# Dequantized weights kept in DRAM as signed bytes, turned into 32-bit numbers on GpSimd

## The chip, the cores and the metric

The kernel runs on one core of a Trainium2 chip. The metric is the device time of one execution in microseconds (us); the profile's span is the time from the first to the last instruction of one profiled execution. A core has these engines, which work side by side, each through its own queue in order: TensorE (PE, the matmuls; its loads of weights are listed as PEld), VectorE (DVE), ScalarE (ACT), GpSimd (POOL), and SyncE (SP), which here issues nearly all DMAs. Matmuls write PSUM, which DVE and ACT read; the DMA engines move data between DRAM and the on-chip memory SBUF.

## The reference

The input is 2048 rows (tokens) of 1024 numbers. A feed-forward block of half weight, a state-space convolution and a second feed-forward block with the same weights follow one another, each behind a normalization and with its input added. The weights are 4-bit numbers, eight in a 32-bit word, with a zero point and a scale for every 128 rows:

```python
w = (qw[:, None, :] >> shifts[None, :, None] & MAXQ).reshape(-1, qweight.shape[1])
z = ((qz[:, :, None] >> shifts[None, None, :] & MAXQ) + 1).reshape(qzeros.shape[0], -1)
Wg, Wu, Wd = [(w - z[g_idx]) * s for each of gate, up, down]
...
x = x + 0.5 * (silu(ln(x) @ Wg) * (ln(x) @ Wu)) @ Wd
x = x + s4_convolution(ln(x))
x = x + 0.5 * (silu(ln(x) @ Wg) * (ln(x) @ Wu)) @ Wd
```

Gate and up are 1024 x 2752 each, down is 2752 x 1024, all in 32-bit floats.

## The kernel before

**Jobs.** The tokens are cut into four blocks of 512. Eight jobs (one block, first or second feed-forward each) run one after another, in the order of `JOBS`. A job has a gate/up stage (`gate_up`, 64 steps) and a down stage (`down`, 44 steps). The convolution of a block is hooked into the steps of the job after its first feed-forward.

**Gate/up.** The 2752 columns are cut into 21 pieces of 128 (the last of 64 columns), and these into eight waves: five of 3 pieces, three of 2. A wave has six accumulators in PSUM (four, or five at the end) and runs over the eight groups of 128 rows: one step is one wave and one group, with a weight tile of 128 x 768 (512 or 640). Each accumulator gets two matmuls a step, since the normalized input is kept as a high and a low part (`pieces`); the matmul of the low part takes the upper 16 bits of each 32-bit weight. After each group the accumulator is multiplied in place by the ratio of that group's scale to the next one's (`scaled`, L539 on ACT or L541 on DVE): this is called an eviction below. At the last group ACT applies silu, DVE multiplies by up (`hf`, a ring of two buffers, L600), and POOL splits the product into a high and a low part (`hh`, L602, and `hl`, L604).

**Down.** Two halves of 512 output columns, each over 22 pieces of rows, with four accumulators and two matmuls for each; evictions as above.

**Weights.** In the first job the packed words are fetched (`fetch`, `fetch_down`), split by DVE into two words of four 4-bit numbers in bytes each (`bytes_of`, L439 and L440), and DVE subtracts the zero points (a table of bf16 numbers, made by `zero_points`, spread to 128 rows by a DMA) from every fourth byte and writes 32-bit numbers `q` (`dequantize`, L454; `dequantize_down`, L486). SP writes `q` to DRAM (`w_q`, `wd_q`; L458, L488). The order of rows changes in this write: word row r holds the weights' rows 8r to 8r + 7. The first tile of all is also gathered directly from `q` by eight DMAs of POOL's queue (L457). `first_weights` hooks this into the steps: wave w is fetched three steps before step 8w - 12, split one step before it, and one eighth of it is dequantized in each step from there; the tiles of down follow from step 52 on into the down stage of job 0.

**Loads.** Every job reads all weight tiles from DRAM again (`load_w`, L523; `load_down`, L531), four steps ahead of use (`AHEAD`), into a ring of eight buffers `w` that is shared with `q`.

**Order.** The framework orders each engine's instructions by its own plan from the order of writing and the dependencies; `in_order_of_writing` forces the written order on named engines, as in `start` (the preparation ahead of the first matmul) and for the splits.

Of the kernel before, what the change touches and what calls it, by code (L numbers as in the profile page):

```python
# [9 lines left out]
F32 = mybir.dt.float32  # L10
BF16 = mybir.dt.bfloat16
F16 = mybir.dt.float16
I32 = mybir.dt.int32
U8 = mybir.dt.uint8
F32R = mybir.dt.float32r
AF = mybir.ActivationFunctionType
ALU = mybir.AluOpType
# [19 lines left out]
STEPS = [(w, g) for w in range(len(WAVES)) for g in range(GK)]  # L37
NH = HID // 512
LIFT = 2.0**20
NST = 64  # L40
# [12 lines left out]
def macaron_s4_kernel(  # L53
# [40 lines left out]
    hpool = ctx.enter_context(tc.tile_pool(name="h", bufs=2 * NF))  # L94
    wpool = ctx.enter_context(tc.tile_pool(name="w", bufs=8))
    gpool = ctx.enter_context(tc.tile_pool(name="g", bufs=3))
# [153 lines left out]
    s_dn = const.tile([P, NC, GD], F32, tag="s_dn", name="s_dn")  # L250
    z_dram = dpool.tile([2 * GK, INTER], BF16, tag="z", name="z_dram")
    zd_dram = dpool.tile([GD, HID], BF16, tag="zd", name="zd_dram")
    ok = const.tile([P, 8], F32, tag="ok", name="ok")
# [19 lines left out]
    def zero_points(which, z):  # L273

        p, n = z.shape
        zi = t2(f"zi_{which}").bitcast(I32)[:p, : 8 * n]
        for k in range(8):
            nc.vector.tensor_scalar(
                zi.rearrange("p (a k) -> p k a", k=8)[:, k, :],
                z,  # L280
                4 * k,
                15,
                ALU.logical_shift_right,
                ALU.bitwise_and,
            )
        tab = t2(f"ztab_{which}").bitcast(BF16)[:p, : 8 * n]
        nc.vector.tensor_scalar(tab, zi, 1.0, None, ALU.add)
        dst, seg, queue = (zd_dram, SEGD, nc.sync) if which else (z_dram, SEG, nc.scalar)
        queue.dma_start(dst.rearrange("g (s n) -> (g s) n", s=seg), tab)
# [15 lines left out]
    def scales(k0, k1, row):  # L305


        n = k1 - k0
        ps = bank(f"ps_s{k0}")
        u0, u1 = 2 * k0, 2 * k1  # L310
        for k in range(n):
            nc.tensor.transpose(
                ps[:, bass.ts(k, 2 * GK)], row[: 2 * GK, bass.ts(k, P)], ident[: 2 * GK, : 2 * GK]
            )
        if k1 == WIDE:
            row = t2("srow_half")
            for m, src in enumerate((gate_s, up_s)):
                nc.sync.dma_start(row[:GK, m * HALF : (m + 1) * HALF], src[:, WIDE * P :])
            nc.tensor.transpose(ps[:, bass.ts(2 * n, GK)], row[:GK, :P], ident[:GK, :GK])
            u1 = UNITS  # L320
        s = s_gu[:, u0:u1]
        flat = lambda a: a.rearrange("p u g -> p (u g)")
        nc.vector.tensor_copy(flat(s), ps[:, : (u1 - u0) * GK])
        inv = t2(f"inv_{k0}")[:, : (u1 - u0) * GK]
        inverse(inv, flat(s), k0)
        own = rat[:, u0:u1]
        inv = inv.rearrange("p (u g) -> p u g", g=GK)
        nc.vector.tensor_tensor(own[:, :, : GK - 1], s[:, :, : GK - 1], inv[:, :, 1:], ALU.mult)
        nc.vector.tensor_scalar(
            own[:, :, GK - 1 :], s[:, :, GK - 1 :], 1.0 / LIFT, None, ALU.mult  # L330
        )

    def scales_down():
# [16 lines left out]
        )  # L350
        nc.vector.tensor_scalar(ratd[:, :, GD - 1 :], s_dn[:, :, GD - 1 :], 0.5, None, ALU.mult)

# [43 lines left out]
    def units(w):  # L396
# [5 lines left out]
    w_q = [  # L402
        dpool.tile([HID, width_of(w)], F32, tag=f"wq{w}", name=f"wq{w}") for w in range(len(WAVES))
    ]
    wd_q = [dpool.tile([INTER, 512], F32, tag=f"wdq{a}", name=f"wdq{a}") for a in range(NH)]

# [11 lines left out]

    first_tile = wpool.tile([P, width_of(0)], F32R, tag="w", name="w_0_0")
    packed = {}  # L420
    NIBBLES = 0x0F0F0F0F

# [7 lines left out]
    def fetch_zeros(w):  # L430
        z = t2(f"z_{w}").bitcast(BF16)[:, : width_of(w)]
        for own, i, lo, hi in columns(w):
            src = z_dram[GK * i : GK * i + GK, lo:hi]
            nc.sync.dma_start(z[:, own], src.unsqueeze(1).to_broadcast([GK, 16, hi - lo]))
        packed[w][1] = z

    def bytes_of(raw, even):

        nc.vector.tensor_scalar(even, raw, NIBBLES, None, ALU.bitwise_and)  # L439
        nc.vector.tensor_scalar(raw, raw, 4, NIBBLES, ALU.logical_shift_right, ALU.bitwise_and)  # L440
        view = lambda a: a.bitcast(U8).rearrange("p (n k) -> p k n", k=4)
        return view(even), view(raw)

    def split(w):
        raw = packed[w][0]
        even = t4(f"even_{w}").bitcast(I32)[:, : width_of(w)]
        packed[w][0] = bytes_of(raw, even)

    def dequantize(w, j):

        parts, z = packed[w]
        q = wpool.tile([P, width_of(w)], F32R, tag="w", name=f"q_{w}_{j}")
        src = parts[j % 2][:, j // 2, :]
        nc.vector.tensor_tensor(q, src, z, ALU.subtract)  # L454
        dst = w_q[w].rearrange("(r j) n -> j r n", j=8)[j]
        if w == 0:
            nc.gpsimd.dma_start(first_tile[j:P:8].bitcast(F32), q[: P // 8].bitcast(F32))  # L457
        nc.sync.dma_start(dst, q.bitcast(F32))  # L458
        if j == 7:
            packed.pop(w)  # L460

    def fetch_down(a, rt):
# [4 lines left out]
        nc.sync.dma_start(both[:, 0], down_qw[rt * P : rt * P + n, cs])  # L467
        z = t4(f"zd_{a}_{rt}").bitcast(BF16)[:n, :512]
        g0 = 8 * rt
# [8 lines left out]
    def split_down(a, rt):  # L478
        both, z = packed[a, rt]
        packed[a, rt] = (bytes_of(both[:, 0], both[:, 1]), z)  # L480

    def dequantize_down(a, rt, j):
        parts, z = packed[a, rt]
        n = z.shape[0]
        q = wpool.tile([P, 512], F32R, tag="w", name=f"qd_{a}_{rt}_{j}")[:n]
        nc.vector.tensor_tensor(q, parts[j % 2][:, j // 2, :], z, ALU.subtract)  # L486
        rows = wd_q[a][8 * P * rt : 8 * P * rt + 8 * n]
        nc.sync.dma_start(rows.rearrange("(r j) n -> j r n", j=8)[j], q.bitcast(F32))  # L488
        if j == 7:
            packed.pop((a, rt))  # L490

    def first_weights(up, dn, at):


        for w in range(1, len(WAVES)):
            s0 = 8 * w - 12
            if w > 1:
                both = lambda w=w: (fetch(w), fetch_zeros(w))
                at(up, s0 - 3, lambda both=both: in_order_of_writing(both, ET.SP))
                at(up, s0 - 1, lambda w=w: in_order_of_writing(lambda: split(w), ET.DVE))  # L500
            else:
                at(up, 0, lambda: in_order_of_writing(lambda: split(1), *STARTING))
            for j in range(8):
                s = s0 + j if w > 1 else j // 2
                at(up, s, lambda w=w, j=j: dequantize(w, j))
# [9 lines left out]

    AHEAD = 4

    def load_w(j, s):
        if j == s == 0:
            return first_tile  # L520
        w, g = STEPS[s]
        t = wpool.tile([P, width_of(w)], F32R, tag="w", name=f"w_{j}_{s}")
        nc.sync.dma_start(t.bitcast(F32), w_q[w][bass.ts(g, P), :])  # L523
        return t

    def load_down(j, a, f):

        t = wpool.tile([P, 512], F32R, tag="w", name=f"wd_{j}_{a}_{f}")
        m = width(f)
        for o in range(0, P, m):  # L530
            nc.sync.dma_start(t[o : o + m].bitcast(F32), wd_q[a][f * P : f * P + m, :])  # L531
        return t

# [9 lines left out]
    def gate_up(j, b, hooks):  # L543
        hi, lo = pieces[b]
        ps = {}
        ready = {s: load_w(j, s) for s in range(AHEAD)}
        for s, (wi, g) in enumerate(STEPS):
            if s + AHEAD < len(STEPS):
                ready[s + AHEAD] = load_w(j, s + AHEAD)
            for hook in hooks.get(s, ()):  # L550
                hook()
            w = ready.pop(s)
            fs = WAVES[wi]
# [9 lines left out]
            for k, pos, done in turns:  # L563
# [18 lines left out]
                if g < GK - 1:  # L582
                    on_act = unit % 2 == 0 or (j == 0 and pos == 1)
                    if unit == 2 * WIDE:
# [37 lines left out]
    def down(j, b, hooks):  # L622

        steps = [(a, f) for a in range(NH) for f in range(NF)]
        ready = {d: load_down(j, *steps[d]) for d in range(AHEAD)}
        for d, (a, f) in enumerate(steps):
            if d + AHEAD < len(steps):
                ready[d + AHEAD] = load_down(j, *steps[d + AHEAD])
            for hook in hooks.get(d, ()):
                hook()  # L630
            w = ready.pop(d)
            if f == 0:
                ps = [acc(f"po_{j}_{a}_{c}") for c in range(4)]
            for c in range(4):
                for k, part in enumerate(reversed(h[f])):
# [7 lines left out]
                    )  # L643
                on_act = c % 2 == 0 or (j == 0 and c == 1 and f % 4 < 3)
                if f < GD - 1:
# [648 lines left out]
    def start():  # L1294
# [19 lines left out]
        moments(0, 1, then)  # L1314
        deviations(0, 1, -LIFT)
        for i in range(8):
            dequantize(0, i)
# [100 lines left out]
```

## Time and profile before

| what | us |
|---|---|
| median of three runs | 2207.82 (2206.94 to 2211.19) |
| the profiled execution's own time | 2209.4 |
| its span | 2207.6 |
| first matmul of job 0 | 29.3 |
| job 0, gate/up and down | 204.5 and 103.9 |
| job 1 to job 7 | 292.2, 277.2, 248.0, 248.0, 274.8, 274.7, 242.0 |

Jobs 1, 2, 5 and 6 hold the convolutions, job 1 also the making of its tables. Busy over the span: PE 2114.3 us (96%), PEld 1420.1, DVE 1702.9 (77%), ACT 1428.7 (65%), POOL 368.1 (17%). The core read 306.86 MB from DRAM and wrote 50.73 MB. In the profile's tables a row names the line, the engine, the operation and `out<-in`, then the count, the busy time and the mean duration. "w<-wq" is a load of a gate/up weight tile, "wd<-wdq" of a down tile, "pg" and "po" are the accumulators of the two stages. A busy PE need not be at its peak, since matmuls overlap; the pace of its steps tells more.

### The profile page before, as it was taken

The numbers are of one execution on the slowest core, as the hardware profiler recorded it, in microseconds if no ns is written. First come the engines' busy times: TensorE is split into PE (matmuls) and PEld (weight loads), VectorE is DVE, ScalarE is ACT, GpSimd is POOL, SyncE is SP. The second block draws the span as 40 slices with busy tenths as digits, with TensorE's granted clock in tenths as the row PEclk, the third lists the DMA queues.
The fourth block names the chain that finished last, engine by engine and source line by source line (L and its number), as shares of the span: only waits on it lengthen the run. The fifth ranks groups of instructions, "written<-read, shape, count | busy, mean of one in ns | idle before, by whom it ended". The sixth has DMA issues, their size and how long they took to land.

```text
span 2207.6 us, 28034 instructions
## 1 busy us (share of the span) xinstructions
PE 2114.3 (96%) x9524; PEld 1420.1 (64%) x9524; DVE 1702.9 (77%) x2803; ACT 1428.7 (65%) x2245; POOL 368.1 (17%) x389
## 2 busy tenths in 40 slices
PE   5888889999999999999999999999999999999998
PEld 3444565566877658755686558776587765865576
DVE  7777969777786877777877787867778677777776
ACT  5667777555764577666766667646676467766665
POOL 0223301222011230122102220112201122012310
PEclk9999999999999999999999999999999999999999
DMA  7768775434453545644655454534455354564443
GB/s 249 248 225 271 242 255 165 140 108 157 134 158 115 171 135 155 193 145 119 208 163 174 127 172 134 158 115 153 138 137 154 115 177 136 155 194 146 133 131 119
DMA packets 163669, 359.93 MB, mean 163 GB/s; under 512 B 22395, under 2 KB 27572, under 8 KB 163518
## 3 DMA queue, kind: packets, MB, share of 16 engines
q1 hardware_dynamic: 162670, 356.50, 52.1%
q8 instruction: 78, 1.28, 0.2%
q10 hardware_dynamic: 592, 1.16, 0.1%
q0 software_dynamic: 256, 0.39, 0.1%
q14 instruction: 73, 0.60, 0.1%
HBM read 306.86 MB, written 50.73 MB: 162 GB/s over the span
## 4 chain that ended last, share of the span: by engine, by line
PE 73%; issue 7%; DVE 5%; POOL 2%; ACT 1%; DVEq 0%; POOLq 0%; ACTq 0%
PE pg L572 42%; PE po L636 24%; PE pc L934 3%; PE pc L915 1%; POOL hl L604 1%; DVE pg L541 1%; PE pb L658 1%; PE pt L215 1%; DVE hf L600 1%; DVE po L541 1%; POOL hh L602 1%; PE st L215 1%; DVE qd L486 0%; PE s_k L854 0%; ACT g L597 0%
## 5 line engine op out<-in xcount | busy, mean ns | idle before, releaser
L539 ACT ACTIVATE pg<-pg,rat 128x512 f32<-128x512 f32 x1264 | 799.9, 661 | 489.3 <-PE pg L572 487.5
L541 DVE TENSOR_TENSOR pg<-pg,rat 128x512 f32<-128x512 f32 x1144 | 761.5, 694 | 180.9 <-PE pg L572 176.1
L572 PE MATMUL pg<-xTh,w 128*128 128x512 f32 x2752 | 874.2, 444 | 12.4 <-DVE pg L541 9.9
L572 PE MATMUL pg<-xTl,w 128*128 128x512 f16 x2752 | 737.8, 384 | 32.7 <-DVE pg L541 14.5
L572 PEld LDWEIGHTS pg<-xTh,w 128*128 128x128 f32 x2752 | 522.4, 190 | 192.6 <-DVE pg L541 24.3
L636 PE MATMUL po<-hl,wd 128*128 128x512 f32 x1344 | 540.5, 403 | 15.7 <-DMA wd<-wdq 7.5
L539 ACT ACTIVATE po<-po,ratd 128x512 f32<-128x512 f32 x670 | 438.1, 662 | 162.5 <-PE po L636 161.8
L636 PE MATMUL po<-hh,wd 128*128 128x512 f32 x1344 | 525.3, 392 | 0.0
L541 DVE TENSOR_TENSOR po<-po,ratd 128x512 f32<-128x512 f32 x610 | 420.9, 698 | 99.2 <-PE po L636 95.4
L572 PEld LDWEIGHTS <-w 128*128 128x128 bf16 x2752 | 227.8, 99 | 370.4 <-issue 186.1
L602 POOL CAST hh<-hf 128x512 fp32r<-128x512 f32 x168 | 109.4, 651 | 1530.7 <-DVE hf L600 976.1
L636 PEld LDWEIGHTS po<-hl,wd 128*128 128x128 f32 x1344 | 253.0, 188 | 92.1 <-DVE po L541 19.7
L636 PEld LDWEIGHTS po<-hh,wd 128*128 128x128 f32 x1344 | 253.6, 189 | 46.3
L604 POOL TENSOR_TENSOR hl<-hf,hh 128x512 fp32r<-128x512 f32 x168 | 222.9, 1327 | 13.4
L600 DVE SCALAR_TENSOR_TENSOR hf<-pg,rat,g 128x512 f32<-128x512 f32 x168 | 124.3, 749 | 90.6 <-ACT g L597 42.8
L597 ACT ACTIVATE g<-pg,rat 128x512 f32<-128x512 f32 x168 | 110.8, 687 | 48.7 <-PE pg L572 38.5
L178 DVE BATCH_NORM_STATS2 stats<-x 128x6 f32<-128x512 f32 x96 | 63.6, 677 | 1.1
L215 PE MATMUL pt<-ident,xn 128*128 128x128 f32 x256 | 42.6, 283 | 11.0 <-ACT xn L1286 11.0
L238 DVE TENSOR_TENSOR xTl<-pt,xTh 128x512 f16<-128x512 f32 x56 | 38.4, 690 | 14.2 <-ACT xTh L237 13.4
L660 DVE TENSOR_TENSOR x<-x,pb 128x512 f32<-128x512 f32 x64 | 43.2, 679 | 6.2 <-PE pb L658 6.0
L215 PEld LDWEIGHTS pt<-ident,xn 128*128 128x128 f32 x256 | 33.1, 145 | 21.8 <-ACT xn L1286 12.8
L237 ACT CAST xTh<-pt 128x512 fp32r<-128x512 f32 x56 | 33.0, 590 | 18.8 <-PE pt L215 18.6
(151 smaller groups left out, 816.9 us busy)
## 6 DMA issues: line engine op xcount, KB each, us to landing
w<-wq SPq DMA_DIRECT2D x319, 384.0 KB
wd<-wdq SPq DMA_DIRECT2D x336, 256.0 KB
w<-wq SPq DMA_DIRECT2D x128, 256.0 KB
w<-wq SPq DMA_DIRECT2D x64, 320.0 KB
x<-in_L_attn_u_dram SPq DMA_DIRECT2D x30, 512.0 KB
wq<-q SPq DMA_DIRECT2D x40, 384.0 KB
wdq<-qd SPq DMA_DIRECT2D x32, 256.0 KB
xs<-x SPq DMA_DIRECT2D x16, 512.0 KB
```

The costliest lines, as they stand in the source:

```text
L178: nc.vector.bn_stats(stats[:, t, i, :], x[b][t][:, bass.ts(i, 512)])
L215: nc.tensor.transpose(ps[:, bass.ts(k, P)], n[:, bass.ts(k, P)], ident)
L539: nc.scalar.activation(dst, src, AF.Copy, scale=sc)
L541: nc.vector.tensor_tensor(dst, src, sc.to_broadcast([P, TB]), ALU.mult)
L572: nc.tensor.matmul(p, weights, (lo, hi)[k][:, g, :], start=(g == 0 and not done), stop=(g == GK - 1 and done), skip_group_check=True,)
L597: nc.scalar.activation(g, pg, AF.Silu, scale=rat[:, 2 * f, GK - 1 :])
L600: nc.vector.scalar_tensor_tensor(hf, pu, last, g, ALU.mult, ALU.mult)
L602: nc.gpsimd.tensor_copy(hi, hf)
L604: nc.gpsimd.tensor_tensor(lo, hf, hi.bitcast(F32), ALU.subtract)
L636: nc.tensor.matmul(ps[c], w[:, bass.ts(c, P)], part, start=(f == 0 and k == 0), stop=(f == NF - 1), skip_group_check=True,)
L660: nc.vector.tensor_tensor(part, part, ps, ALU.add)
L934: nc.tensor.matmul(dst, lhsT, rhs, start=start, stop=stop, skip_group_check=True)
```

## The change

**Bytes.** `w_q` and `wd_q` hold signed bytes instead of 32-bit floats. A byte is eight times (weight minus zero point): -128 to 120. The factor 8 is taken out of the last group's scale (`EIGHT`).

**Zero points in packed form.** The table in DRAM holds 32-bit words whose four bytes each are 120 - 8 * z (z without the 1), so that bit patterns add without a carry. `bytes_of` leaves each 4-bit number in bits 3 to 6 of its byte. The new `signed` adds table and word as 16-bit numbers on DVE, and flips each byte's top bit with an exclusive-or; `take_zeros` and `split_down` call it for both halves of a tile. What is left for `dequantize` is to pick every fourth byte into a contiguous `q`: on POOL, and for six of the eight picks of wave 0 on DVE.

**Conversion.** A load now brings bytes (`load_bytes`, ring of six buffers `b`, four steps ahead, across stages and jobs), and `make_weights`, three steps ahead, turns them into 32-bit numbers (`w`, now a ring of five): on POOL, except the very first tile (DVE) and, in the gate/up stage of job 0, the groups 1, 2 and 5 (ACT).

**Evictions of job 0.** Those that had been given to ACT beyond the even ones are cut: of the unit at place 1 in gate/up only groups 0 and 4 stay on ACT, and in down none of unit 1.

```diff
-    wpool = ctx.enter_context(tc.tile_pool(name="w", bufs=8))
+    wpool = ctx.enter_context(tc.tile_pool(name="w", bufs=5))
+    bpool = ctx.enter_context(tc.tile_pool(name="bytes", bufs=6))
+    qpool = ctx.enter_context(tc.tile_pool(name="q", bufs=4))
...
-        tab = t2(f"ztab_{which}").bitcast(BF16)[:p, : 8 * n]
-        nc.vector.tensor_scalar(tab, zi, 1.0, None, ALU.add)
+        tab = t2(f"ztab_{which}").bitcast(I32)[:p, : 8 * n]
+        nc.vector.tensor_scalar(
+            tab.bitcast(U16).rearrange("p (n k) -> p n k", k=2),
+            zi.unsqueeze(2).to_broadcast([p, 8 * n, 2]),
+            -8.0 * 257,
+            120.0 * 257,
+            ALU.mult,
+            ALU.add,
+        )
...
-    first_tile = wpool.tile([P, width_of(0)], F32R, tag="w", name="w_0_0")
+    first_tile = bpool.tile([P, width_of(0)], I8, tag="b", name="b_0_0")
...
-    NIBBLES = 0x0F0F0F0F
+    NIBBLES = 0x78787878
...
-        z = t2(f"z_{w}").bitcast(BF16)[:, : width_of(w)]
+        z = t4(f"z_{w}").bitcast(I32)[:, : width_of(w)]
...
-        nc.vector.tensor_scalar(even, raw, NIBBLES, None, ALU.bitwise_and)
-        nc.vector.tensor_scalar(raw, raw, 4, NIBBLES, ALU.logical_shift_right, ALU.bitwise_and)
-        view = lambda a: a.bitcast(U8).rearrange("p (n k) -> p k n", k=4)
-        return view(even), view(raw)
+        nc.vector.tensor_scalar(even, raw, 3, NIBBLES, ALU.logical_shift_left, ALU.bitwise_and)
+        nc.vector.tensor_scalar(raw, raw, 1, NIBBLES, ALU.logical_shift_right, ALU.bitwise_and)
+        return even, raw
+
+    def signed(part, z):
+        both = part.bitcast(U16)
+        nc.vector.tensor_tensor(both, both, z.bitcast(U16), ALU.add)
+        nc.vector.tensor_scalar(both, both, 0x8080, None, ALU.bitwise_xor)
+        return part.bitcast(I8).rearrange("p (n k) -> p k n", k=4)
...
-        q = wpool.tile([P, width_of(w)], F32R, tag="w", name=f"q_{w}_{j}")
-        src = parts[j % 2][:, j // 2, :]
-        nc.vector.tensor_tensor(q, src, z, ALU.subtract)
+        q = qpool.tile([P, width_of(w)], I8, tag="q", name=f"q_{w}_{j}")
+        engine = nc.vector if w == 0 and j % 3 < 2 else nc.gpsimd
+        engine.tensor_copy(q, packed[w][j % 2][:, j // 2, :])
...
-        q = wpool.tile([P, 512], F32R, tag="w", name=f"qd_{a}_{rt}_{j}")[:n]
-        nc.vector.tensor_tensor(q, parts[j % 2][:, j // 2, :], z, ALU.subtract)
+        q = qpool.tile([P, 512], I8, tag="q", name=f"qd_{a}_{rt}_{j}")[:n]
+        nc.gpsimd.tensor_copy(q, src)
...
+    LOAD, MAKE = 4, 3
...
+    def make_weights(i):
+        j, stage, s = queue[i]
+        b = loaded.pop(i)
+        made[i] = t = wpool.tile(list(b.shape), F32R, tag="w", name=f"w_{stage}_{j}_{s}")
+        if i == 0:
+            nc.vector.tensor_copy(t, b)
+        elif j == 0 and stage == "up" and s % GK in (1, 2, 5):
+            nc.scalar.copy(t, b)
+        else:
+            nc.gpsimd.tensor_copy(t, b)
...
+    def next_weights():
+        i = at_use[0]
+        at_use[0] += 1
+        for k in range(LOAD) if i == 0 else ():
+            load_bytes(k)
+        for k in range(MAKE) if i == 0 else ():
+            make_weights(k)
+        if i + LOAD < len(queue):
+            load_bytes(i + LOAD)
+        if i + MAKE < len(queue):
+            make_weights(i + MAKE)
+        return made.pop(i)
...
-                    on_act = unit % 2 == 0 or (j == 0 and pos == 1)
+                    on_act = unit % 2 == 0 or (j == 0 and pos == 1 and g % 4 == 0)
...
-                on_act = c % 2 == 0 or (j == 0 and c == 1 and f % 4 < 3)
+                on_act = c % 2 == 0
...
         deviations(0, 1, -LIFT)
+        take_zeros(0)
         for i in range(8):
             dequantize(0, i)
```

## The prediction

> **What bounds the kernel now.** I read the strips of the page first, then the busy times by stage, then who TensorE (PE) waited for, then the costs of single instructions.
>
> ```profile
> PEclk9999999999999999999999999999999999999999
> DMA  7768775434453545644655454534455354564443
> ```
>
> DMA is at 6 to 8 tenths in the first six of 40 slices (55 us each) and at 3 to 6 afterwards: the first job, which also makes the weights, is another regime. So I cut the span at the jobs, whose bounds I found by counting matmuls in the timeline.
>
> ```profile
> core 0: us, PE busy (x) PEld busy (x) DVE busy (x) ACT busy (x) POOL busy (x), PEclk, DMA share, GB/s
> 0.00:29.30 29.30, 5.33 (x24) 3.86 (x25) 22.27 (x65) 12.41 (x19) 4.78 (x15) 0.92 0.70 231
> 29.30:233.80 204.50, 177.44 (x727) 98.00 (x728) 154.99 (x230) 143.95 (x236) 46.68 (x40) 0.95 0.75 253
> 233.80:337.70 103.90, 93.24 (x393) 68.42 (x393) 81.92 (x143) 74.35 (x122) 22.59 (x19) 0.97 0.75 241
> ...
> 907.10:1155.00 247.90, 244.29 (x1097) 162.25 (x1096) 192.54 (x304) 169.24 (x266) 39.33 (x42) 1.00 0.53 164
> ```
>
> Rows: preparation, gate and up of job 0, down of job 0, and the whole of job 3 with the same matmuls. Job 0 takes 308.4 us, job 3 247.9 us, of which PE is busy 244.3: later jobs are at PE's own pace (2.70 us for a step of 12 matmuls, 1.81 for one of 8). What can be won lies almost all in job 0: its first stage 204.5 against 162.6 in job 3 (some 3 us of the difference are job 0's own transposes), its second 103.9 against 85.6, so about 39 + 18 = 57 us. The waits of PE in job 0 (29.2 to 337.7), and after it:
>
> ```profile
> PE pg L572 <- DMA w<-wq: 13.9, 11, 3.8
> PE pg L572 <- DVE pg L541: 9.9, 7, 4.0
> PE po L636 <- DMA wd<-wdq: 7.5, 3, 5.0
> PE po L636 <- DVE po L541: 3.3, 7, 1.3
> PE pg L572 <- DMA w<-q: 2.7, 1, 2.7
> ```
> ```profile
> PE pg L572 <- DVE pg L541: 14.5, 25, 2.1
> ```
>
> Total us, times, longest. In job 0 the weights' DMAs hold PE for 13.9 + 7.5 = 21.4 us, VectorE (DVE) for 13.2; in the other seven jobs no DMA holds PE. The clock lost 0.05 x 204.5 + 0.03 x 103.9 = 13.3 us more: after the stop that ends at 134.4 us (3.5 us) the next twelve matmuls take 5.2 us in place of 2.7.
>
> **What one instruction costs.**
>
> ```profile
> L454 DVE TENSOR_TENSOR q<-even,z x32: 676/948/2021, 16.6 to 202.5; 128x768 fp32r<-128x768 uint8 x20, 128x512 fp32r<-128x512 uint8 x8, 128x640 fp32r<-128x640 uint8 x4
> L439 DVE TENSOR_SCALAR rawd<-rawd x6: 413/422/1503, 189.3 to 280.4; 128x512 int32<-128x512 int32 x4, 88x512 int32<-88x512 int32 x2
> L602 POOL CAST hh<-hf x168: 603/612/1346, 58.0 to 2115.2; 128x512 fp32r<-128x512 f32 x168
> L604 POOL TENSOR_TENSOR hl<-hf,hh x168: 1263/1280/2305, 58.7 to 2115.9; 128x512 fp32r<-128x512 f32 x168
> L730 DVE TENSOR_TENSOR s_cos<-s_dr 128x1024 f32<-128x1024 f32 x1 | 1.2, 1219 | 0.0
> ```
>
> ns min/median/max (the last row: busy us, mean ns).
>
> **1. Bytes in DRAM.** A gate/up tile falls from 384 to 96 KB, a down tile from 256 to 64, written once and read eight times. In job 0 every step reads and writes one, so most of the 253 GB/s goes. The 21.4 us of DMA waits go, and I credit about 60% of the lost clock to them (21.4 of some 35 us of waits): -8. In jobs 1 to 7 the gain is nothing: no DMA wait is there. Price: -29.4.
>
> **2. Conversion to 32 bits, added, mostly on GpSimd (POOL).** No row converts bytes. Nearest is the one-input cast: 0.612 us for 512 columns. From L604 (1.28 for 512) and L927 (1.00 for 384 columns, two inputs) an instruction has a fixed part near 0.18 us, so a cast runs at 0.84 ns a column: 0.83 us for 768. The other end is the two-input slope, 2.15 ns a column: 1.83 us.[...] A wave of eight steps in job 0 has 5 conversions and 8 byte picks on POOL and three pairs of casts at 1.89: by the row 13 x 0.83 + 5.7 = 16.5 us of PE's 21.6[...]. I take the row: one input, one output. In later jobs 8 x 0.83 + 5.7 = 12.3 of 21.6.
>
> Latency: in job 3 the last hl of a wave ends 8.46 us after the wave's last step begins; the conversion queued behind it is needed 11.3 us after, 9.3 where the next wave has 4 units. With 0.6 to 0.9 us it is in time. POOL's casts stand in the same queue: a conversion in front of hh and hl delays hl, and the two hf buffers pass that to DVE:
>
> ```profile
> DVE hf L600 <- POOL hl L604: 33.9, 29, 1.4
> ```
>
> That wait exists already. I take +1 us for all later jobs; the upper end is one conversion per wave on this path (second rival). A late conversion stops PE; a conversion on ScalarE (ACT; g = 1, 2, 5 of job 0, about 0.9 us) that waits for its bytes stops the evictions queued behind it. SP's order lends cover: loads are bound only by six byte buffers, each free once converted, except in job 0, where the load stands behind writes that wait for POOL's picks.
>
> **3. DVE in job 0.** Leaves: 56 + 48 subtractions, 56.2 + 38.1 = 94.3 us in the groups of that stretch. Comes: per half of each packed tile an add and an exclusive-or on 16-bit words, twice the columns. The row [...](L730: 1.22 for 1024) makes the add of 1536 words 1.75 us[...]; no row here shows 16-bit words, so both ends stay: over 7 waves and 6 down tiles 32 us[...] or 57 us. I take 32[...]. Evictions moved from ACT to DVE: 5 of 7 in each of 8 waves = 40, and 34 in down, 74 x 0.694 = 51. Contention: L439 goes from 422 to 1503 and L454 from 948 to 2021 where POOL works[...]. With POOL busy some 195 of 283 us (69 now, about 127 of new work at 0.84 ns a column and 0.18 us each), 80 such instructions wait about 0.25 us each (half a cast, two times in three): +20. Sum: -94 + 32 + 51 + 20 = +9. DVE was busy 237 of 308 us and would be 246 of about 283: it becomes the limit of job 0, and its 13.2 us of waits stay. I add +3 for the tighter fit.
>
> ACT loses 74 x 0.663 = 49 us and gains 22 to 24 conversions of 0.7 to 0.9: no limit.
>
> **4. Start.** The first matmul waits on this chain:
>
> ```profile
> 16.62 0.96 DVE L454 TENSOR_TENSOR q<-even,z 128x768 fp32r<-128x768 uint8 x1
> ...
> 29.29 1.44 PE L572 MATMUL pg<-xTl,w 128*128 128x512 f16 x3 [2.69 <-DMA w<-q]
> ```
>
> The zero table gets 688 outputs[...], +0.5; its 32-bit broadcast doubles those bytes, hidden behind bn_stats on DVE; add and or for two halves +2.9 to +5.4; eight subtractions of 0.87 become six copies of 0.55 to 0.95 on DVE, -3.7 to -1.3, two go to POOL, whose eight DMA issues (0.5 each) queue behind them; converting the first tile +0.5 to +0.95. Ends +0.2 and +5.6; I take +2.5.
>
> **Sum.** -29.4 + 1 + 3 + 2.5 = -22.9 on a span of 2207.6, whose run took 2209.4; the median is 2207.8, so the span stands for it: 2185, rounded to 2184.
>
> **Rivals.** *Job 0 reaches PE's pace*: conversions hide, DVE's words are cheap[...]: -57 + 2.5 gives 2153. For it: ACT has room, POOL is at 70%. Against: DVE at 246 of 253 us would need no gap. *POOL decides* (slower): at 1.22 us per 768 columns 13 conversions and picks plus casts fill 21.6 us. At 1.83, job 0 grows by 5 x 7.9 + 2 x 5.9 + 6 in its first stage and about 36 in down over a 253 us floor: 346, +38; later jobs lose about 2 us each at wave ends: 2260. The same end comes if conversions stand before hh and hl: 0.6 us in 56 waves = 34 us, which with the gain gives 2218. *DVE takes it all*: the 16-bit words run at the slow end (+25): 271 us of work in job 0 at 87% is 311: 2213. *Nothing moves*: the waits change from DMA to DVE at equal length: about 2207.
>
> **Chances.** Likeliest (2165 to 2200) 0.50; PE's pace 0.20; DVE takes it all 0.08; nothing moves 0.08; POOL decides 0.14. Range 2150 to 2232 leaves the far POOL case and a little below. About 4.4 us (0.2%) can be told from no change: faster 0.74, same 0.07, slower 0.19, a few of the "nothing" cases falling on either side.
>
> **What would show it.** Right: no PE wait on weight DMAs in job 0; DMA strip at 2 to 4; the conversion of 768 columns near 0.83 us; job 3 still near 248. Wrong: PE waiting for POOL's w after a wave's end, hf waiting longer for hl, the 16-bit add above 1.2 us, or first matmul after 35 us.

## The result, and the profile after

The changed kernel took 2196.07 us (median of four runs, 2195.57 to 2197.09), the kernel before 2208.9 (2206.94 to 2211.19): a ratio of 0.9939, 95% interval 0.9927 to 0.9952. The span of the profiled execution went from 2207.6 to 2193.7 us. About half of the forecast gain came. The repeated executions of one kernel differ in the clock granted to PE (a mean of 0.987 to 0.994 over the span in 23 executions of the kernel before, with times of 2204.3 to 2215.5 us), so a stage taken from one profile can hold a little more or less of lowered clock than another. The DMA strip of the page (PEclk is 9 in every slice, as before), and the stages, cut at the matmuls as before (preparation, gate/up of job 0, down of job 0, job 1, job 3):

```profile
DMA  4433321112111211211321121112111121121111
```
```profile
core 0: us, PE busy (x) PEld busy (x) DVE busy (x) ACT busy (x) POOL busy (x), PEclk, DMA share, GB/s
0.00:28.80 28.80, 4.65 (x19) 3.39 (x19) 19.90 (x54) 11.21 (x17) 7.16 (x17) 1.00 0.51 171
28.80:204.90 176.10, 170.55 (x732) 95.45 (x732) 149.72 (x255) 137.27 (x221) 127.48 (x161) 0.99 0.39 115
204.90:313.00 108.10, 97.06 (x395) 69.62 (x394) 91.94 (x176) 59.58 (x93) 63.97 (x89) 0.95 0.28 87
313.00:612.70 299.70, 291.64 (x1318) 196.59 (x1317) 240.56 (x409) 174.31 (x272) 121.41 (x158) 0.98 0.16 49
892.80:1140.10 247.30, 244.71 (x1097) 162.23 (x1096) 193.58 (x304) 169.35 (x266) 114.28 (x151) 1.00 0.20 61
```

Gate/up of job 0 fell from 204.5 to 176.1 us and its clock rose from 0.95 to 0.99. Down of job 0 *rose* from 103.9 to 108.1, although its DMA share fell from 0.75 to 0.28. Over the whole span, from the exact ends of the stages:

| part | change, us |
|---|---|
| before the first matmul | -0.5 |
| gate/up of job 0 | -28.4 |
| down of job 0 | +4.2 |
| gate/up of job 1, of job 2 | +7.0, +2.4 |
| down of jobs 1 to 7 (0.45 to 0.6 each) | +3.8 |
| gate/up of the other later jobs | -2.3 |
| after the last matmul | -0.2 |

The first two give 28.9 us, the rest takes back 15.0. The longest waits of PE in job 0 (total us, times, longest), then, from the groups by shape (busy us, mean ns), POOL's conversion and the 16-bit add in gate/up:

```profile
PE pg L628 <- DVE w_up L572: 6.6, 1, 6.6
PE pg L628 <- DVE pg L600: 3.3, 9, 0.6
PE pt L219 <- DVE xn L212: 2.7, 1, 2.7
PE po L689 <- DVE po L600: 2.7, 6, 1.1
PE po L689 <- ACT po L598: 2.1, 6, 0.6
PE po L689 <- DVE s_vc L758: 1.9, 1, 1.9
PE pg L628 <- POOL w_up L576: 1.5, 2, 0.8
PE po L689 <- POOL w_down L576: 1.4, 1, 1.4
```
```profile
L576 POOL CAST w_up<-b 128x768 fp32r<-128x768 int8 x304 | 255.7, 841 | 438.3 <-PE pg L628 337.5 <-issue 47.3 <-PE po L689 32.3
...
L461 DVE TENSOR_TENSOR even<-even,z 128x1536 uint16<-128x1536 uint16 x5 | 4.8, 952 | 0.8 <-DMA z<-z_dram 0.8
```

No weight DMA holds PE any more (6.6 is the start's own chain). In down, however, other stops have taken the place of the DMA's: `xn` (the normalized input of the next block, which PE transposes), evictions of DVE and of ACT, `s_vc` (one of the convolution's tables) and a conversion, 10.8 us in sum, where the weights' DMAs and the evictions had made 11.7 before. PE's busy time there grew from 93.2 to 97.1 us, at a clock of 0.95 in place of 0.97. Why down did not become shorter is the question for the experiments.

### The profile page after: what moved, and what is told of

It is laid out like the page before. It is cut to its first block, busy times and chain, and to the rows that moved or that the text cites. A ratio compares the mean times of both kernels' runs of the same rounds, so it can differ in the third digit from the quotient of the medians.

```text
span 2193.7 us, 29717 instructions
## 1 busy us (share of the span) xinstructions
PE 2119.6 (97%) x9524; PEld 1421.1 (65%) x9524; DVE 1720.4 (78%) x2826; ACT 1404.9 (64%) x2197; POOL 1015.0 (46%) x1334
## 3 DMA queue, kind: packets, MB, share of 16 engines
q8 instruction: 77, 1.26, 0.2%
## 4 chain that ended last, share of the span: by engine, by line
PE 84%; DVE 7%; POOL 4%; issue 2%; DMA 1%; SPq 1%; ACT 0%; POOLq 0%; DVEq 0%; ACTq 0%
PE pg L628 50%; PE po L689 26%; PE pc L987 3%; DVE pg L600 2%; PE pc L968 1%; PE pb L711 1%; POOL hl L660 1%; PE pt L219 1%; DVE po L600 1%; DVE hf L656 1%; POOL w_up L576 1%; PE st L219 1%; POOL w_down L576 1%; POOL hh L658 1%; DVE rawd L461 0%
## 5 line engine op out<-in xcount | busy, mean ns | idle before, releaser
L600 DVE TENSOR_TENSOR pg<-pg,rat 128x512 f32<-128x512 f32 x1184 | 788.0, 694 | 167.5 <-PE pg L628 163.2
L628 PE MATMUL pg<-xTh,w_up 128*128 128x512 f32 x2752 | 878.5, 444 | 11.9 <-DVE pg L600 9.4
L628 PE MATMUL pg<-xTl,w_up 128*128 128x512 f16 x2752 | 731.1, 384 | 14.7 <-DVE w_up L572 6.6
L576 POOL CAST w_up<-b 128x768 fp32r<-128x768 int8 (+2 forms) x487 | 376.0, 774 | 614.0 <-PE pg L628 470.6
L628 PEld LDWEIGHTS pg<-xTh,w_up 128*128 128x128 f32 x2752 | 519.7, 190 | 203.0 <-DVE pg L600 41.7
L689 PE MATMUL po<-hl,w_down 128*128 128x512 f32 x1344 | 540.6, 405 | 15.4 <-DVE po L600 9.7
L689 PE MATMUL po<-hh,w_down 128*128 128x512 f32 x1344 | 523.6, 393 | 0.0
L600 DVE TENSOR_TENSOR po<-po,ratd 128x512 f32<-128x512 f32 x640 | 441.6, 698 | 93.6 <-PE po L689 89.1
L628 PEld LDWEIGHTS <-w_up 128*128 128x128 bf16 x2752 | 228.3, 99 | 344.1 <-issue 165.2
L576 POOL CAST w_down<-bd 128x512 fp32r<-128x512 int8 x352 | 220.6, 628 | 422.3 <-PE po L689 366.2
L689 PEld LDWEIGHTS po<-hl,w_down 128*128 128x128 f32 x1344 | 252.9, 189 | 94.1 <-DVE po L600 23.9
L689 PEld LDWEIGHTS po<-hh,w_down 128*128 128x128 f32 x1344 | 254.0, 189 | 46.0
L660 POOL TENSOR_TENSOR hl<-hf,hh 128x512 fp32r<-128x512 f32 x168 | 218.0, 1297 | 7.9
```

The source lines that it names most:

```text
L576: nc.gpsimd.tensor_copy(t, b)
L600: nc.vector.tensor_tensor(dst, src, sc.to_broadcast([P, TB]), ALU.mult)
L628: nc.tensor.matmul(p, weights, (lo, hi)[k][:, g, :], start=(g == 0 and not done), stop=(g == GK - 1 and done), skip_group_check=True,)
L660: nc.gpsimd.tensor_tensor(lo, hf, hi.bitcast(F32), ALU.subtract)
L689: nc.tensor.matmul(ps[c], w[:, bass.ts(c, P)], part, start=(f == 0 and k == 0), stop=(f == NF - 1), skip_group_check=True,)
```

## The experiments

Each kernel is the changed one with the edit shown. Ratios are against the kernel before, on the same chip. One caution holds for all: the framework plans the order of instructions anew for each variant, and stages that an edit does not touch move with it. From here on a stage or job is counted to the end of its last matmul, which makes down of job 0 108.2 us and job 1 299.9 in the changed kernel. Where no edit touched it and `hf` had two buffers, down of job 0 took 106.7 to 108.6 us in three kernels, but job 1 296.0 to 301.7 in five. (The run with the traffic, left out of this band, adds copies in job 0 alone and still had 307.6 in job 1.) A stage is read against these bands. As to whole times, the intervals of the first two runs and of the run on the tables' order overlap the changed kernel's 0.9927 to 0.9952; those of the two runs that take work off POOL in down do not.

### Is it the evictions moved to DVE?

```diff
-                on_act = c % 2 == 0
+                on_act = c % 2 == 0 or (j == 0 and c == 1 and f % 4 < 3)
```

> Only the evictions of job 0's down stage go back to ScalarE as before the change (34 of them). Theory (VectorE is the bound of that stage, since the change gave it these evictions[...]): down of job 0 falls from 108.1 us to about 100, the span by about 8 us to 2186. Rival (that stage waits for GpSimd's queue, picks and conversions being late): it stays within 2 us of 108.

2190.1 us, ratio 0.9905 (0.9875 to 0.9935); down of job 0 106.3 us. That is 2 us less, at the edge of the band, not the 8 that the theory of overfull evictions wants, and within the rival's 2 us. The test is not clean, though: the new plan also put more of job 1's table instructions into DVE's queue in this stage (15.8 us in place of 7.3), and PE's waits there for DVE's evictions rose from 2.7 to 11.0 us. So the theory is not supported, and not refuted either.

### Are job 1's conversions on POOL what makes it longer?

```diff
-        elif j == 0 and stage == "up" and s % GK in (1, 2, 5):
+        elif (j == 0 and stage == "up" and s % GK in (1, 2, 5)) or (
+            j == 1 and stage == "up" and s < 44
+        ):
             nc.scalar.copy(t, b)
```

> Conversions of job 1's gate/up steps 0 to 43 (while the convolution's tables are made on VectorE) go to ScalarE in place of GpSimd. Theory[...]: job 1 falls by about 6 us from 299.7, its small VectorE operations e, r and s_work fall back from 16.6 us in sum to about 10, and the GpSimd hl operations go back to 1.28 us. Rival (job 1 lost its 7 us because the tables' instructions are planned in another order): no change beyond 2 us.

2191.64 us, ratio 0.9917 (0.9887 to 0.9947); job 1 297.8, 2 us less. Inconclusive: inside the band. The theory's own signs hardly came either: in job 1 the small instructions on `e`, `r` (128x4) and `s_work` (128x8) fell from 16.4 to 14.7 us, not to 10 (11.0 before the change), those on `r` stayed at 3.8, and the slowest `hl` still took 2.33 us. The same edit was tried again on another base below.

### Is the packed form needed?

```diff
-EIGHT = 8.0
+EIGHT = 1.0
...
-        packed[w] = [signed(part, z) for part in parts]
+        pass
...
-        engine = nc.vector if w == 0 and j % 3 < 2 else nc.gpsimd
-        engine.tensor_copy(q, packed[w][j % 2][:, j // 2, :])
+        nc.vector.tensor_tensor(q, parts[j % 2][:, j // 2, :], z, ALU.subtract)
```

Bytes and conversions stay; DVE subtracts a bf16 table from each eighth, as before the change.

> Bytes in DRAM and conversion as in the changed kernel, but the zero points are subtracted by VectorE byte by byte as before (112 instructions with 0.95 or 0.68 us), in place of the packed add and exclusive-or (52 instructions in the steps of job 0, 49 us) and GpSimd's picks. Theory (VectorE bounds job 0): 40 us more on VectorE, job 0 grows from 284 us to 305 to 325. Rival (job 0 is bound by GpSimd's queue or by DMA): job 0 stays at 280 to 290, or falls since GpSimd has 70 us less.

2212.57 us, ratio 1.0013 (1.0005 to 1.0021); job 0 190.1 + 115.0 us. The stretch of job 0:

```profile
26.60:331.80 305.20, 272.52 (x1125) 156.78 (x1125) 273.25 (x463) 196.69 (x315) 128.21 (x145) 0.98 0.31 92
```

DVE is busy for 273 of 305 us, against 241.7 of 284.3 in the changed kernel. So bytes without the packed form gain nothing with these evictions: the packed form is worth 0.0074 of the time, some 16 us.

### Does the traffic matter?

```diff
+    def extra(i):
+        n = 576 if queue[i][1] == "up" else 384
+        for k in range(2):
+            r = ((2 * i + k) % 16) * P
+            nc.sync.dma_start(extra_dram[k, i, :, :n], u[r : r + P, :n])
...
+        if queue[i][0] == 0:
+            extra(i)
```

Two unused copies from DRAM to DRAM per step of job 0, about the bytes that the change had saved.

> The changed kernel with two copies inside DRAM added to each step of job 0 (295 KB each in gate/up, 197 KB in down), which brings the DMA engines' bytes back to those of before; nobody waits for them. Theory (the weights' traffic was what held TensorE): TensorE waits for loads again and job 0 grows by 15 to 30 us from 284. Rival (the gain came from the other division of work between the engines): under 5 us.

2265.91 us, ratio 1.0245 (1.0212 to 1.0277). The two stages of job 0, then PE's waits there:

```profile
34.50:247.60 213.10, 176.00 (x731) 97.92 (x731) 149.95 (x252) 139.62 (x222) 119.56 (x150) 0.95 0.81 246
247.60:374.90 127.30, 100.03 (x392) 74.35 (x392) 90.51 (x146) 58.89 (x91) 65.62 (x97) 0.89 0.70 201
```
```profile
PE po L698 <- POOL w_down L576: 28.8, 15, 7.5
PE pg L637 <- POOL w_up L576: 19.9, 7, 5.8
```

The DMA share is back near 0.75 (0.81 and 0.70), the clock back at 0.95 and below, and job 0 is 56 us longer. Sign right, size missed: 15 to 30 had been expected. Each such copy reads and writes DRAM and stands in SP's queue ahead of a byte load, so it is more than a restoration. The reading to keep: a late DMA is now booked under POOL, whose conversions in turn waited 32.6 + 23.5 us for their bytes in this job; the name of the releaser changes, the cause does not.

### Is it POOL beside DVE in down?

POOL has two kinds of new or old work in down of job 0: the conversions, and the turn of the next block (`xTh`, `xTl`, L238 and L239), which the kernel gave to POOL in job 0 already before. One run takes each away.

```diff
-        elif j == 0 and stage == "up" and s % GK in (1, 2, 5):
+        elif j == 0 and (stage == "down" or s % GK in (1, 2, 5)):
             nc.scalar.copy(t, b)
```

> The 44 conversions of job 0's down stage go from GpSimd to ScalarE (busy 60 of 108 us there, then about 87). Theory (VectorE's packed add and exclusive-or of the down tiles, means 1.09 and 0.83 us against minima of 0.68 and 0.41, wait for GpSimd[...], and the evictions behind them hold TensorE): their means fall below 0.9 and 0.65, and down of job 0 falls from 108 to about 101. Rival (only the lump of these instructions ahead of the evictions counts, whatever GpSimd does): means and stage stay within 2 us.

2189.92 us, ratio 0.9902 (0.9885 to 0.9918); down of job 0 100.8, as the theory wants. Its signs came only by half: the exclusive-or's mean fell from 829 to 660 ns, but the add's rose from 1090 to 1168.

```diff
-                pool = j == 0
+                pool = False
```

> In the down stage of job 0 the transposed input's two parts are made by ScalarE and VectorE as in the other jobs (8 more VectorE instructions of 0.69 us) in place of GpSimd's cast and two-input subtraction (17.6 us). Theory[...]: the means of the packed add and exclusive-or of down fall by 0.1 us or more each, and the stage stays within 3 us of 108 since VectorE gets 5.5 us more and 3 to 5 us of waits less. Rival (no conflict): means unchanged, the stage 4 to 6 us longer.

2188.22 us, ratio 0.9897 (0.988 to 0.9913); down of job 0 98.9, although DVE and ACT got *more* to do. That is below the range expected. The 16-bit add (L461) and exclusive-or (L462) of the down tiles, ns min/median/max, first in the changed kernel, then with the turn taken off POOL:

```profile
L461 DVE TENSOR_TENSOR rawd<-rawd,zd x12: 677/1092/1764, 175.3 to 268.0; 128x1024 uint16<-128x1024 uint16 x8, 88x1024 uint16<-88x1024 uint16 x4
L462 DVE TENSOR_SCALAR rawd<-rawd x12: 411/806/1497, 177.8 to 268.9; 128x1024 uint16<-128x1024 uint16 x8, 88x1024 uint16<-88x1024 uint16 x4
```
```profile
L461 DVE TENSOR_TENSOR rawd<-rawd,zd x12: 674/683/1698, 175.6 to 262.2; 128x1024 uint16<-128x1024 uint16 x8, 88x1024 uint16<-88x1024 uint16 x4
L462 DVE TENSOR_SCALAR rawd<-rawd x12: 410/420/934, 177.8 to 263.1; 128x1024 uint16<-128x1024 uint16 x8, 88x1024 uint16<-88x1024 uint16 x4
```

The minima agree, the medians of 1092 and 806 fall to 683 and 420 (the means, 1090 and 829, to 902 and 550, by more than the theory asked). So the exclusive-or, which has one input, became longer with the turn on POOL as the two-input add did. In the timeline of the changed kernel (start us, us) this looks as follows, between two evictions (L600):

```profile
235.01 0.68 DVE L600 TENSOR_TENSOR po<-po,ratd 128x512 f32<-128x512 f32 x1
235.61 0.90 DVE L454 TENSOR_SCALAR rawd<-rawd 128x512 int32<-128x512 int32 x1
...
236.43 2.11 DVE L461 TENSOR_TENSOR rawd<-rawd,zd 128x1024 uint16<-128x1024 uint16 x2
...
237.96 3.11 POOL L239 TENSOR_TENSOR xTl<-turn,xTh 128x512 f16<-128x512 f32 x2
238.46 2.90 DVE L462 TENSOR_SCALAR rawd<-rawd 128x1024 uint16<-128x1024 uint16 x2
...
241.28 1.09 DVE L212 TENSOR_SCALAR xn<-x,mv,r 128x1024 f32<-128x1024 f32 x1
...
242.29 0.69 DVE L600 TENSOR_TENSOR po<-po,ratd 128x512 f32<-128x512 f32 x1
```

The same two adds and two exclusive-ors with the turn taken off POOL:

```profile
235.74 1.28 DVE L461 TENSOR_TENSOR rawd<-rawd,zd 128x1024 uint16<-128x1024 uint16 x2
236.95 0.75 DVE L462 TENSOR_SCALAR rawd<-rawd 128x1024 uint16<-128x1024 uint16 x2
```

They take 2.0 us there and 5.0 us beside the turn. `xn` stands behind them in DVE's queue, and PE, which transposes it, stops for 2.72 us until 242.52 (the wait for `xn` in the list of PE's waits above); without the turn on POOL this wait is 0.2 us. So the cause of this stop is shown.

It is not the whole of the stage. In the profile of the changed kernel PE's clock is at one half from 242.5 to 245.9 us, just behind that stop, and again from 256.2 to 259.6 and from 300.5 to 303.9: 5.1 us are lost. Down of job 0 in five kernels, with PE's busy time, what the stage took beyond it, the clock, and the longest stretch between two evictions on DVE:

| kernel | stage, us | PE busy | beyond | clock | longest stretch |
|---|---|---|---|---|---|
| before | 104.0 | 93.4 | 10.7 | 0.97 | 9.8 |
| changed | 108.2 | 97.2 | 11.0 | 0.95 | 6.6 |
| conversions off POOL | 100.8 | 91.3 | 9.5 | 0.98 | 7.8 |
| turn off POOL | 98.9 | 91.8 | 7.1 | 1.00 | 4.9 |
| tables in order (next run) | 103.5 | 91.4 | 12.1 | 1.00 | 6.9 |

With the turn off POOL 3.9 of the 9.3 us are fewer stops, and 5.4 are PE's busy time, about what the clock gave back. With the conversions off it the stop for `xn` is even longer (3.5 us), and so is the longest stretch without an eviction; its gain is mostly PE's busy time, and by which way the conversions act on it is not separated. Nor does every stop bring a lowered clock: the next run keeps the stop of 2.7 us and has none. What decides the clock stays open. It was not tried what the two edits give together.

### The order of the table's instructions

```diff
-                    at(up, s, lambda: next(tables, None))
+                    at(up, s, lambda: in_order_of_writing(lambda: next(tables, None), ET.DVE))
```

> The changed kernel, with the convolution's tables' VectorE instructions held in the written order, so that none of them is planned into job 0's down stage. Theory A (the order of the tables' instructions, moved up by the new plan, costs job 1 its 7 us and job 0's down stage part of its time): job 1 falls from 299.7 to about 293, down of job 0 from 108.1 to about 104. Theory B (job 1 loses to GpSimd's conversions[...], whatever the order): job 1 stays at 297 or more.

2190.42 us, ratio 0.9918 (0.9901 to 0.9936). Down of job 0 103.5, 4.8 less and below the band: 34 of DVE's table instructions, which belong to job 1, had been planned into job 0's down (7.3 us), and PE's stop of 1.9 us for `s_vc` is gone with them. But by the table above the gain is all in PE's busy time, at a clock of 1.00; the time beyond it even grew. Job 1 did not gain (301.4), so the early planning is not seen to lengthen job 1.

### What the conversion costs in later jobs

```diff
-            nc.gpsimd.tensor_copy(t, b)
+            for _ in range(2 if j in (1, 2, 3) else 1):
+                nc.gpsimd.tensor_copy(t, b)
```

> In jobs 1, 2 and 3 every conversion on GpSimd is done twice (GpSimd busy about 190 of 247 us in job 3). Theory (GpSimd's time is hidden[...]): job 3 grows by 1 to 4 us at the wave ends, job 1 with its many two-input VectorE instructions by 5 us or more. Rival (the loss of later jobs is GpSimd's queue): job 3 grows by over 10 us like job 1.

2207.99 us, ratio 0.9987 (0.998 to 0.9994). Job 1, then job 3, with each conversion made twice:

```profile
313.70:618.40 304.70, 292.94 (x1317) 196.73 (x1316) 246.20 (x409) 174.59 (x272) 200.12 (x266) 0.98 0.16 48
902.80:1152.30 249.50, 245.08 (x1098) 162.28 (x1097) 195.48 (x304) 169.46 (x266) 187.05 (x256) 1.00 0.20 61
```

By the exact ends, 73 to 79 us of POOL work more cost job 3 2.1 us, but job 1 5.0 (304.9, above the band) and job 2 4.3. So the price is not POOL's time. DVE's busy time, for the same number of instructions, grew by about as much as the job: from 240.6 to 246.2 us in job 1 and from 193.6 to 195.5 in job 3. And `hf` waited hardly longer for `hl` (38.1 us in all, 37.5 in the changed kernel), which speaks against the queue in front of `hl`. The price is paid where DVE has the convolution's small and wide instructions as well. A piece of job 1 from the timeline of the changed kernel (start us, us) shows the interplay:

```profile
339.48 2.38 POOL L660 TENSOR_TENSOR hl<-hf,hh 128x512 fp32r<-128x512 f32 x1
...
339.50 1.22 DVE L786 TENSOR_TENSOR s_sq<-s_sin 128x1024 f32<-128x1024 f32 x1
...
340.64 1.24 DVE L204 SCALAR_TENSOR_TENSOR r<-e,r 128x4 f32<-128x4 f32 x1
...
342.50 1.26 POOL L660 TENSOR_TENSOR hl<-hf,hh 128x512 fp32r<-128x512 f32 x1
342.56 1.22 DVE L205 TENSOR_SCALAR r<-r 128x4 f32<-128x4 f32 x1
...
344.44 0.38 PE L628 MATMUL pg<-xTl,w_up 128*128 128x512 f16 x1 [1.92 <-DVE pg L600]
```

`hl` takes 2.38 us instead of 1.26 while DVE's wide instruction runs; then DVE's four-column instructions, 0.15 to 0.17 us elsewhere, take 1.24 and 1.22 while POOL is in `hl`, and each ends with that `hl`. Evictions come late and PE stops for 1.92 us. In this piece the partner is `hl`, which POOL had before the change, and not a conversion.

### POOL too slow: the second rival made real

```diff
-        nc.vector.tensor_scalar(both, both, 0x8080, None, ALU.bitwise_xor)
...
-            nc.gpsimd.tensor_copy(t, b)
+            nc.gpsimd.tensor_scalar(t, b, -128.0, None, ALU.add)
```

The exclusive-or is left out; the bytes are unsigned and the conversion subtracts 128, on DVE and ACT likewise.

> The exclusive-or is left out: the bytes stay unsigned with an offset of 128, and the conversion subtracts it (one-input tensor_scalar on GpSimd and VectorE, bias on ScalarE). VectorE loses 26 instructions in the steps of job 0, 23.5 us. Theory (VectorE with its waits bounds job 0): job 0 falls from 284 to about 272 and the first matmul comes 1 us earlier; later jobs unchanged if GpSimd does tensor_scalar at the pace of the cast (0.83 us for 768 columns). Rival (job 0 is bound elsewhere): under 3 us. If the instruction takes GpSimd twice as long, later jobs grow by 2 us each.

2299.01 us, ratio 1.0397 (1.0379 to 1.0414). Far from expected: job 0 was to fall to 272 us and took 321, and jobs 1 to 3 grew by 8 to 13 us each, not by 2.

```profile
L576 POOL TENSOR_SCALAR w_up<-b 128x768 fp32r<-128x768 uint8 x304 | 650.4, 2149 | 151.5 <-PE pg L628 118.8 <-POOL w_up L576 16.3 <-PE po L689 5.7
```
```profile
PE pg L628 <- DVE pg L600: 65.1, 46, 6.4
PE po L689 <- DVE po L600: 36.0, 15, 5.1
```

The first fence is the group of the conversion, the second PE's waits. The added constant makes POOL's conversion 2149 ns in place of 841. PE's waits are booked under DVE, yet DVE lost work: its `hf` waits 78.7 us for POOL's `hl` (37.5 in the changed kernel), and evictions stand behind `hf` in DVE's queue.

### A third buffer for hf

```diff
-    qpool = ctx.enter_context(tc.tile_pool(name="q", bufs=4))
+    qpool = ctx.enter_context(tc.tile_pool(name="q", bufs=3))
...
-    hfpool = ctx.enter_context(tc.tile_pool(name="hf", bufs=2))
+    hfpool = ctx.enter_context(tc.tile_pool(name="hf", bufs=3))
...
-                pool = j == 0
+                pool = False
```

> The kernel with the turn on VectorE, with three hf buffers in place of two (and three q in place of four, to make room). Theory (hf waits for hl behind GpSimd's casts, 37 us in all, and a part reaches TensorE at the wave ends): job 3 falls from 247.1 to about 243, the span by 10 to 20 us. Rival (that wait is hidden): within 3 us.

2169.23 us, ratio 0.9819 (0.9803 to 0.9835), by the ratios some 17 us under the same kernel with two `hf` buffers (0.9897, on another chip). First a line of VectorE's waits in the changed kernel, then the group of `hf` in this one, with the idle time before it after the last bar:

```profile
DVE hf L656 <- POOL hl L660: 37.5, 37, 2.1
```
```profile
L656 DVE SCALAR_TENSOR_TENSOR hf<-pg,rat,g 128x512 f32<-128x512 f32 x168 | 123.0, 749 | 52.7 <-ACT g L653 45.6 <-POOL qd L510 2.2 <-POOL q L478 0.8
```

The wait for `hl` is gone. Job 3 goes to 244.6 us, job 1 to 294.6 and the down stages of the later jobs to 85.5, where they had been before the change. Job 3 is now 3.6 us better than *before* the change, and `hf` had waited 33.9 us for `hl` there already, so a good part of this gain is not a repair of the change but was open all along; the kernel before was not run with three buffers. The `q` ring, shortened to make room, was not tried alone.

### Job 1's conversions on ACT, again

The edit of the second run was put on the kernel with the turn taken off POOL, with two `hf` buffers and then with three.

> The turn on VectorE and the conversions of job 1's steps 0 to 43 on ScalarE together. [...]job 1 falls from 301.5 to about 295; by the run with the second edit alone, which brought 2 us there and 2 in job 2, the sum is about 2184 us.

2180.66 us, ratio 0.9874 (0.9857 to 0.989); job 1 296.8, against 301.5 without it: -4.7, the size expected, yet within the band of job 1. The whole time does not settle it either, since its interval overlaps that of the kernel without the second edit (0.988 to 0.9913). It supports the theory, that job 1 loses to its conversions on POOL, without proving it.

> Turn on VectorE, three hf buffers, and job 1's conversions of steps 0 to 43 on ScalarE together. If the three effects add, 2169 less the 4 to 5 us that the third edit brought to job 1 beside the turn: about 2165 us. If hf's third buffer already hides what the conversions cost in job 1, it stays at 2169.

2170.73 us, ratio 0.982 (0.9802 to 0.9837): no better than with the buffer alone. Job 1 itself took 292.8, against 294.6. With two buffers the edit went with 4.7 us less in job 1, with three with 1.8. That would fit a third buffer which already removes most of what the conversions cost there, but both differences are within job 1's band, so it is not shown.

## Why the prediction was half right

**Right: direction, and the first stage.** Waits and clock of job 0 were priced at -29.4; gate/up alone gained 28.4, more than its share of that term (13.9 of the 21.4 us of waits, and about 6 of the 8 for the clock). The rest came where the prediction had said that nothing moves: PE's waits for DVE's evictions there fell from 9.9 to 3.3 us, and the clock's loss from 10.2 to 0.01 x 176 = 1.8. 13.9 + 6.6 + 8.4 = 28.9. The copies of traffic (fourth experiment) support it: with the bytes back, clock and stops come back. That job 0 as a whole came out at -24.2, near the -26.4 of its terms, is luck: gate/up gave over 8 us more than the waits and the clock booked for it, and down some 13 less.

**Right: POOL's price.** The conversion took 841 ns (forecast 0.83 us), 628 for 512 columns; the row of the one-input cast decided well against the two-input slope, whose end was 1.83 us. With one constant added, in the run without the exclusive-or, the same conversion took 2149 ns, more than even that end.

**Right in sum: DVE in job 0.** 149.7 + 91.9 = 241.6 us, forecast 246. The add of 1536 words took 0.95 us, the exclusive-or 0.62 and 0.68 (means of the two halves). No row of the kernel before showed an add or an exclusive-or of 16-bit words; L439 took 422 ns for 512 columns, L730 1219 for 1024, and that the new words would be fast enough for 32 us in sum was the author's estimate. That DVE would be the limit of job 0 with its 13.2 us of waits was not right: its evictions held PE for 3.3 + 2.7 us.

**Start.** +2.5 was forecast, -0.5 came: tile copies on DVE at 0.54 to 0.72 us, the conversion at 0.56, near their low ends. The zero table, forecast as an estimate at +0.5, took 0.52 us in place of 0.34. Seven kernels with two `hf` buffers and this same start had their first matmul at 28.9 to 30.4 us, so the half microsecond itself says little.

**Wrong: down of job 0.** Its waits of 7.5 us and its clock were booked as gain, and +3 as the loss to a tighter fit; the stage lost 4.2 instead. The step that failed is that a stop taken away is time won: `xn`, `s_vc`, a conversion and ACT's evictions took the DMA's place, PE's time beyond its busy time went from 10.7 to 11.0 us, and the clock fell to 0.95 where a gain was booked. The term "contention, +20", spread evenly as a quarter of a microsecond for each of 80 instructions, had the wrong shape, though DVE's whole work came out near: four packed instructions in a row lost 3 us beside the turn, and `xn` behind them held PE for 2.72. The prediction counted POOL's new work there, but did not look at what of its old work, the two-input turn, stood beside the new 16-bit operations; the 1503 ns that it quotes for L439 lies at 261.4 us, beside just such an `xTl`. The runs with the turn off POOL (-9.3 us) and with the conversions off it (-7.5) show that POOL's work is the place; of the first, 3.9 us are stops and the rest goes with the clock, of which no run shows what sets it.

**Wrong: "+1 us for all later jobs".** It was +11.0. The prediction named the path, a conversion near `hl` and two `hf` buffers, but took latency alone: is the conversion in time? It is; no conversion is among PE's waits there. Doubling the conversions shows a price that latency leaves out, DVE's own instructions becoming longer (+5.0 us in job 1, +4.3 in job 2, +2.1 in job 3). That this is also what the change itself cost job 1 is only argued: with the conversions of job 1's steps 0 to 43 off POOL the small instructions stayed slow. `hf`'s wait for `hl`, the path that the prediction named, grew only from 33.9 to 37.5 us in all; three buffers take away both the old part and the new. How much of job 1's 7.0 us is this lengthening beside POOL and how much the newly planned order stays open: the waits booked on PE for DVE evictions there grew from 1.8 to 6.0 us in total, its time at half clock from 6.8 to 10.2 us (1.7 us lost), and job 1 lay at 296.0 in one run that did not touch it.

**Rivals.** PE's pace in job 0 was not reached (gate/up 176.1 against 162.6). POOL did not decide at 841 ns; at 2149 it did, at 2299 us, beyond the 2260 forecast for 1.83.

## What to carry to other kernels

When work is moved to GpSimd, price it twice: by its own duration, and by what its instructions do to VectorE's beside them (here two 16-bit adds and two exclusive-ors took 5.0 us in place of 2.0, a four-column instruction 1.24 in place of 0.15); a sum of busy times hides the second. When a stop of the bottleneck is taken away, ask which stop is next. When a stage is slower than its sum, look at what the bottleneck stopped for and at its clock; a single suspicious stretch explains its own stop (2.72 us here), and a table of several kernels shows how much of the stage that is. A ring of two between two engines can pass a delay of the one to the other (`hf` waited 37.5 us in all for `hl`); a third buffer, with a `q` ring one shorter, was worth some 17 us here, more than the whole change.

## What the hardware showed unexpectedly

On GpSimd a cast of 768 bytes to 32 bits took 841 ns, the same with one constant added 2149 ns. Side by side, VectorE's instructions and GpSimd's each became longer, and not in proportion to their size: a four-column VectorE instruction (L204) went from 0.15 to 1.24 us, a GpSimd subtraction of 512 columns (L660) from 1.26 to 2.38. In the down stage of job 0 of the changed kernel the lowered clock came in three stretches of 3.4 us at one half; a stop of PE of 2.7 us was followed by one there, and by none in the run with the tables in order.
